# The last of sixteen token blocks finished in two halves, with new orders for the last two blocks

## The chip, the cores and the metric

The kernel runs on one core of a Trainium2 chip, in one launch. The metric is the device time of an execution in microseconds (us); smaller is better. Engines are named as the profile names them: PE is TensorE (matrix products and transposes), PEld its weight loads, DVE is VectorE, ACT is ScalarE, POOL is GpSimd, and SP issues the plain DMAs.

## The reference

The input x is 128 sequences of 64 tokens with 256 features. Four residual steps follow one another:

```python
x = x + attention(x, cond)        # 16 heads, keys = queries = values from one projection, modulated by cond
x = x + adapter(x, cond)          # returns up + its input, so this step gives 2 x + up
x = x + fuse(x, ids, cond, ...)   # layer norms with per-token tables, W1 (silu), W2, layer norm
x = x + decoded(x, cond)          # per sequence: x @ (U V) + bias, U (256 x 30) decoded from cond
```

The change touches the end of the third step and the fourth step:

```python
h = jax.nn.silu(s @ W1 + b1) @ W2 + b2
return _ln(h, g, b)               # added to x, which then goes through the fourth step
...
out = jnp.einsum('bsd,bde->bse', x, weight) + bias[:, None, :]
```

All arithmetic of these parts is in fp32.

## The kernel before, in words

**Blocks and tiles.** The 8192 tokens are cut into 16 blocks of 512 tokens (8 sequences), numbered 0 to 15, each of 4 tiles of 128 tokens. Each block goes through `attention` (lines 842 to 993, with `tile_attention` for each tile) and then `rest` (1177 to 1464). Several things are kept transposed, features by tokens: x1T after attention (line 986), x2T after the adapter (1222).

**What `rest` does.** The adapter is two groups of small products (`down`, 1191, and `up`, 1209). Each tile of x2T is transposed back to tokens by features (1259, 1262), normalized (statistics 455 and 456 on DVE; one over the root and the offset on POOL, 460, 462, 1239 and 1240; the normalization itself on ACT, 1245), scaled by a gathered table (1270, 1276), normalized again, and transposed (1294, 1297). Per-token tables are put in through one-hot products (1303, 1312). W1 is 16 products of 512 columns for a block (1330) and one of a table (1339), then silu (1345, 1348), which leaves s2, features by tokens.

From here on the change is at work. W2 gives one product for each tile of 128 tokens (`second`, 1373): DVE adds b2 (1378) and takes the statistics (455, 456); POOL makes ry = (variance + epsilon) to the power -1/2 and nry = - mean times ry for all four tiles at once (460, 462, 1239, 1240); ACT normalizes each tile (1245); POOL scales it and adds x2 (1384, 1387). For the fourth step the normalized tiles are transposed (`turn`, 1399) for each half c of the features. In all blocks but the last an ACT copy with a bias makes x3T of it. In the last block, `quick` is set: the transposes read the normalized tile yn before POOL's scaling, and a DVE scalar_tensor_tensor scales, adds x2T and writes x3T (1405), so that POOL's scaling is beside this path and not on it. `first` (1426) multiplies x3T by the decoded U of each sequence, DVE adds ub and writes zT (1437), `last` (1452) multiplies by V, DVE adds x3 (1460), and SP stores 128 tokens at a time (1464).

**The order of the work.** A planner (class `Plan`, lines 59 to 202) collects all operations of the whole kernel with a guessed duration, their inputs and outputs and the buffers they need, and then lays them out with a list schedule: at each step it takes, on each engine, those operations that could start first (within 0.02 us of the earliest), and of these the one with the smallest number; the emitted program follows this order on every engine. The number comes from a table for each kind of block (`TURNS`, 208 to 308: "prologue", "first", "second", "middle", "last but one", "last"), one number for each operation in the order in which the code lists them, plus 400 for each block:

```python
            picks = []
            for eng, c in best.items():
                first = min(c)[0]
                picks.append(min(((p, n, t) for t, p, n in c if t <= first + 0.02)))
            t, n = min((t, n) for _, n, t in picks)
```

The block before its own `rest` is over shares the engines with the attention of the next block, so the tables of blocks 14 ("last but one") and 15 ("last") decide how the last two blocks lie beside each other. Nothing follows block 15. PE results go to four banks of accumulator memory (kind "bank") and one group of four banks for attention scores. An operation with a new buffer can only be placed when a buffer of that kind is free.

Of the kernel before, what the change touches and what calls it, by code (L numbers as in the profile page):

```python
# [12 lines left out]
AF = mybir.ActivationFunctionType  # L13
ALU = mybir.AluOpType
# [4 lines left out]
C = 2  # L19
T = 512  # L20
# [38 lines left out]
class Plan:  # L59
# [177 lines left out]
    -16938 -30526 -18028 36301 -15547 26405 -802 6729 -39099 -41863 42240 -45014 -14562 -27174 17926 -11891 -33252  # L237
    -15193 -45201 -45201 -45201 -12582 9703 17987 22744 15597 -18168 17424 -28042 -41758 -7357 -451 25437 -8991
    -12614 459 -11776 29958 -7569 23567 -6641 13097 26814 -28106 7375 -575 12318 20069 -38198 23459 -38462 36836
    27311 31943 -4776 26854 -14776 2811 12753 3636 -20535 28655 16056 22892 -31515 6510 -3096 -41775 12301  # L240
    """,
    "second": """
    13400 17649 -18056 -2478 -39796 -25603 -43400 19336 -42575 -24634 15841 18877 1893 18958 3437 12808 907 8003
# [11 lines left out]
    1457 -45077 -25320 -34934 -8032 -37786 -19094 -8437 5339 5339 5339 -12394 -20304 14994 3721 -11664 -7635 -27664  # L255
    27176 20895 26121 9336 -35791 -14043 -7673 8369 -42327 -31969 -25693 17291 2553 -36411 -3402 -15873 13422 7027
    -32778 19435 22712 -20010 12141 -39669 -37660 1149 -27222 -44023 37623 -37115 -18717 26495 3505 18710 -32292 -430
    15236 18791 21609 -17410 29738
    """,
    "middle": """  # L260
    -945 -5006 28741 3275 -555 -2679 4333 19756 13246 29462 3507 42603 5115 -1489 14772 22434 -2133 33481 31798 41815
# [9 lines left out]
    25821 12505 -1402 -5360 3342 27949 30405 6793 33874 -4408 26737 -9042 5014 33335 43087 44838 12803 42849 4251  # L271
    28780 21150 7584 9227 29132 5260 5260 5260 28987 31520 -2237 3828 8090 938 30118 3864 -4871 -7133 4057 30319
    11418 -2268 -597 -6095 7699 -2331 11788 11039 36273 619 1024 4669 34043 16725 5303 33221 -6438 31026 14080 11161
    37456 23037 11095 -11007 27922 -5110 11858 21714 35520 -1388 28909 27611 779 30000 -4851 23042
    """,
    "last but one": """
    -945 -5006 28741 3292 -555 -2679 4333 19756 13246 29426 3507 42507 949 -1489 14772 22434 -2092 33522 31798 41815
    951 30003 36734 39833 31441 44287 36835 36712 48388 -2211 33995 35152 6414 18014 27987 -10794 26523 6071 13167
    215 -9627 40936 -4357 6419 10572 4571 -7266 41550 17576 2454 32076 31767 -2728 16615 41208 837 4340 8765 36154
    -10880 4665 -558 -2062 4662 -3798 1273 31044 36706 35521 -1668 -419 19391 3818 26245 31507 24910 28317 -6286  # L280
    26998 -11618 25996 12900 26677 40415 20947 4197 4591 -10897 34316 29621 46596 6494 -4361 -5325 30488 28382 33266
    18048 33066 30258 -4468 44044 39446 3045 11442 54 3568 3791 -5774 -2389 836 17585 32107 3610 3509 11677 27998
    5918 -289 -3076 10611 22471 8317 24462 31609 27367 -11407 5640 5006 25531 6317 12721 12013 -6353 39363 7446 4072
    -1182 -2303 33420 5842 -3197 -3385 30659 31515 868 756 5023 33464 5290 34805 27086 29256 -2628 -4019 6625 33507
    3780 1799 30520 32280 29029 46575 20997 32367 9369 29333 -3611 1761 5073 23038 -2673 4124 -3837 18828 -210 5311
    32964 13572 -5042 815 27152 -6571 45385 6618 32189 18218 25530 13431 4354 28866 27343 42996 27711 28905 48852
    20499 25821 12505 19373 -5371 3342 27949 30404 6752 33874 -4408 26737 -9042 5014 33335 43087 44864 12794 42849
    4268 28770 21167 7601 9132 29149 5277 5277 5277 29004 31538 -2220 3845 8107 955 30135 3881 -4854 -7113 4074 30336
    11443 -2251 -580 -6078 4549 -2314 4266 11515 36765 1109 1500 5145 34519 17201 5779 33709 -5975 31030 14097 11178
    37473 23054 11112 -11491 27939 12681 11926 21735 35542 -1369 28928 27461 806 30077 -4774 23069  # L290
    """,
    "last": """
    -918 -4932 28785 3332 -569 37576 95 19583 13303 29612 3564 42657 5172 -1432 14778 22470 -2127 33487 31798 41753
    970 30025 36750 39866 31463 44309 36857 36734 48399 29838 33987 35461 6445 18036 28009 -10772 26548 6113 13077
    237 -9611 40952 -4341 6378 10566 11434 -7289 41527 17553 -2664 32185 32004 -2665 16815 41408 1037 4540 8965 36354
    -10831 4624 -604 -2085 4601 -3493 1256 17026 36681 35506 -1449 -434 19376 3801 25885 18811 24911 28352 -6303
    26981 -11699 25941 12883 26660 40398 20930 37525 4574 -10945 34299 29411 46591 6473 3726 -5383 30451 28410 33294
    18120 33105 30216 -4508 44002 39404 2964 11361 -166 3348 3579 -5994 -2333 610 18563 31899 3363 3325 4560 27779
    5744 -463 -3063 10622 -5376 8328 24473 31758 33518 -11396 5316 4677 43337 5936 12777 11684 -6037 39679 7352 3989
    -1170 -2067 33534 5696 -3081 -3304 30916 3513 1082 969 -1348 33586 5412 34403 27208 29378 -11701 -4005 6612 27354  # L300
    3767 1811 -9041 32275 33374 46570 20992 32362 9366 29381 -3588 1701 5121 4398 17015 4312 -3658 31671 -173 5447
    33077 13685 12794 -1508 27373 -6586 45375 6606 32445 18219 25520 13404 4325 28839 16940 42969 36247 29019 48820
    20465 25794 12337 -1583 -5541 3161 27768 30224 6612 33693 -4589 26551 -9304 4752 33073 42825 44576 12454 42500
    3902 28515 20894 7574 8848 28753 4872 4872 4993 28720 31263 -2335 3579 7833 -1601 29984 3730 -5005 -7186 4016
    30266 11356 -2321 -666 -6056 7806 -2377 11778 11029 36263 589 994 4678 34088 16701 5288 33069 -6488 30973 13881
    11108 37403 22984 11042 -11060 27869 3313 11805 21661 19322 -1441 28856 27558 772 29993 -4858 10564
    """,
}

# [2 lines left out]
def resid_chain(ctx: ExitStack, tc: tile.TileContext, a: dict, out: bass.AP, nblk: int = NBLK):  # L312
# [13 lines left out]
    def over_tokens(ap):  # L326
        return ap.unsqueeze(len(ap.shape)).to_broadcast([*ap.shape, S])
# [105 lines left out]
    def pe(us, f, reads, writes, claims=(), full=1.0, mode=0):  # L433

        op("PE", us + 0.16, f, reads, writes, busy=us, claims=claims, full=full, mode=mode)

    def dve(n, f, reads, writes, more=0.0, pair=False):

        us = 0.085 + n / 960 + more
        op("DVE", us + 0.08, f, reads, writes, busy=us, pair=pair)  # L440

    def act(n, f, reads, writes, more=0.0, table=0):
        us = 0.085 + n / 1200 + more
        op("ACT", us + 0.08, f, reads, writes, busy=us, table=table)

    def pool(us, f, reads, writes):
        op("POOL", us + 0.1, f, reads, writes, busy=us)
# [5 lines left out]
    def stats(x, mv, tl):  # L453
        st = Buf("st")
        dve(256, lambda: nc.vector.bn_stats(st.t, x.t), [x], [st])  # L455
        dve(6, lambda: nc.vector.bn_aggr(mv.t[:, tl, :], st.t), [st], [(mv, tl)])  # L456
# [538 lines left out]
    def tile_attention(b0, tl, xsT, dmk, osT):  # L995
# [178 lines left out]
            [(osT, tl)],  # L1174
        )

    def rest(blk, x1T, pw, oh, wdn, wup, tab, uT):

        b0 = blk * NB
# [62 lines left out]
        def normalize(dst, src, r, nr, tl):  # L1242
            act(
                256,
                lambda: nc.scalar.activation(
                    dst.t, src.t, AF.Identity, bias=nr.t[:, tl : tl + 1], scale=r.t[:, tl : tl + 1]
                ),
                [src, r, nr],
                [dst],
                more=0.186,  # L1250
            )
# [111 lines left out]
        else:  # L1363
            plan.skip(C)
        mvy, ry, nry = Buf("mvy"), Buf("ry"), Buf("nry")
        x3 = [Buf("x3") for _ in range(NTILE)]
        yn = [Buf("h") for _ in range(NTILE)] if quick else x3
        for tl in range(NTILE):
            ps = Buf("bank")

            def second(ps=ps, tl=tl):
                for c in range(C):
                    nc.tensor.matmul(  # L1373
                        ps.t[:, :F], s2.t[:, c, bass.ts(tl, 128)], w2.t[:, c, :], start=(c == 0), stop=(c == C - 1)
                    )
# [4 lines left out]
        rstd(mvy, ry)  # L1380
        offset(mvy, ry, nry)
        for tl in range(NTILE):
            normalize(yn[tl], x3[tl], ry, nry, tl)
            pool(0.65, lambda tl=tl: nc.gpsimd.tensor_tensor(x3[tl].t, yn[tl].t, lg, ALU.mult), [yn[tl]], [x3[tl]])
            pool(
                0.65,
                lambda tl=tl: nc.gpsimd.tensor_tensor(x3[tl].t, x3[tl].t, x2[tl].t, ALU.add),
                [x3[tl], x2[tl]],
                [x3[tl]],
            )  # L1390
# [3 lines left out]
        for c in range(C):  # L1394
            ps = Buf("bank")

            def turn(ps=ps, c=c):
                for tl in range(NTILE):
                    nc.tensor.transpose(ps.t[:, bass.ts(tl, 128)], yn[tl].t[:, bass.ts(c, 128)], ident)  # L1399

            pe(0.5, turn, yn, [ps], [x3T])
            if quick:
                dve(
                    512,
                    lambda ps=ps, c=c: nc.vector.scalar_tensor_tensor(
                        x3T.t[:, c, :], ps.t, lgT[:, c : c + 1], x2T.t[:, c, :], ALU.mult, ALU.add
                    ),
                    [ps, (x2T, c)],
                    [(x3T, c)],
                )  # L1410
                continue
            act(
                512,
                lambda ps=ps, c=c: nc.scalar.activation(x3T.t[:, c, :], ps.t, AF.Identity, bias=lbe[:, c : c + 1]),
                [ps],
                [(x3T, c)],
                more=0.093,
            )
# [171 lines left out]
```

## Time and profile before

| | us |
|---|---|
| median of 3 runs | 899.68 |
| lowest and highest | 899.44, 901.99 |
| the profiled execution, its own time | 902.43 |
| its span, from the first to the last instruction | 900.6 |
| mean granted clock of TensorE | 0.985 |

| engine | busy us | share of the span | instructions |
|---|---|---|---|
| PE | 832.6 | 92% | 9752 |
| DVE | 636.7 | 71% | 1365 |
| POOL | 608.1 | 68% | 826 |
| ACT | 447.6 | 50% | 825 |

The profile belongs to the execution of 902.43 us, so times from its start and durations are compared with its span of 900.6 us; 1.8 us lie outside. The busy times of PE are modelled, and its instructions overlap at their ends. A product in fp32 stands as two PE instructions in the trace. "idle before <- X" names the instruction whose end released a waiting one. The tile names in the trace are those of the memory: x2, x3, h and xn live in slots that show as "uu" or "p", x3T and s2 show as "uu", and b2, lg and vw as "late".

### The profile page before, as it was taken

How to read it: one execution, taken by the hardware profiler on the slowest of the kernel's cores; microseconds unless marked ns; L12 is line 12 of the kernel's file. 1: busy time of each engine (PE TensorE's matmuls, PEld its weight loads, DVE VectorE, ACT ScalarE, POOL GpSimd, SP SyncE). 2: the span in 40 equal slices, each digit the busy share in tenths (PEclk: the TensorE clock that was granted, in tenths of full speed). 3: DMA queues.
4: the chain of work that ended last, by engine and by line, in shares of the span. 5: the costliest groups of instructions: out<-in, count | busy, mean ns of one | idle time of the engine just before them, and what ended most of it. 6: DMA issues, size and time to landing. Idle time of an engine off the chain costs nothing.

```text
span 900.6 us, 23967 instructions
## 1 busy us (share of the span) xinstructions
PE 832.6 (92%) x9752; PEld 535.5 (59%) x9752; DVE 636.7 (71%) x1365; ACT 447.6 (50%) x825; POOL 608.1 (68%) x826
## 2 busy tenths in 40 slices
PE   5869999999999999999999999999999999999884
PEld 3648746656665756656565746656565757565442
DVE  3679867768685877777685868777685858776543
ACT  1454453545564555555455645555454645545241
POOL 4463673949687695949496794949496786945333
PEclk9989999999999999999999999999999999999997
DMA  8768742133423242332324232322324222202000
GB/s 264 191 151 237 253 122 77 56 86 107 126 84 116 68 122 76 94 95 76 116 83 128 66 112 81 92 94 73 115 84 128 77 85 66 82 3 71 1 24 25
DMA packets 62575, 90.24 MB, mean 100 GB/s; under 512 B 6328, under 2 KB 46200, under 8 KB 62464
## 3 DMA queue, kind: packets, MB, share of 16 engines
q1 hardware_dynamic: 57344, 71.92, 27.9%
q0 software_dynamic: 5120, 16.78, 6.0%
q8 instruction: 77, 1.26, 0.6%
q14 instruction: 34, 0.28, 0.1%
HBM read 75.44 MB, written 13.24 MB: 98 GB/s over the span
## 4 chain that ended last, share of the span: by engine, by line
PE 76%; DVE 10%; ACT 7%; issue 3%; POOL 2%; DMA 2%; SPq 0%; DVEq 0%; ACTq 0%; POOLq 0%
PE bank L1330 21%; PE sc L1057 8%; PE bank L1001 7%; PE bank L968 6%; PE bank L1373 6%; PE bank L1132 6%; DVE mt L1066 4%; PE bank L1044 2%; PE sc L1107 2%; PE bank L1162 2%; ACT uu L1297 2%; PE bank L1209 2%; PE bank L1399 2%; PE bank L1303 2%; PE bank L1191 2%
## 5 line engine op out<-in xcount | busy, mean ns | idle before, releaser
L1066 DVE TENSOR_REDUCE mt<-sc 128x8 f32<-128x1024 f32 x128 | 151.8, 1205 | 27.8 <-PE sc L1057 25.3
L1121 ACT ACTIVATE e<-sc 128x1024 f32<-128x1024 f32 x128 | 125.8, 1022 | 78.8 <-PE sc L1107 78.8
L1151 POOL TENSOR_TENSOR att<-ao,rz 128x256 f32<-128x256 f32 x45 | 28.0, 623 | 83.3 <-DVE rz L1148 77.3
L1312 DVE TENSOR_TENSOR uu<-uu,bank 128x512 f32<-128x512 f32 x96 | 63.6, 678 | 14.3 <-PE bank L1303 13.9
L1001 PE MATMUL bank<-wk,xsT 128*128 128x256 f32 x256 | 72.7, 420 | 1.1 <-POOL xsT L911 1.1
L1330 PE MATMUL bank<-uu,w_s 128*128 128x512 f32 x128 | 66.7, 604 | 0.8 <-DVE uu L1312 0.8
L1330 PE MATMUL bank<-x2T,w_x 128*128 128x512 f32 x128 | 64.7, 608 | 0.0
L1330 PE MATMUL bank<-uu,w_t 128*128 128x512 f32 x128 | 63.4, 604 | 0.5 <-DVE uu L1312 0.5
L1373 PE MATMUL bank<-w,uu 128*128 128x256 f32 x256 | 61.8, 385 | 1.9 <-DVE uu L1348 1.9
L1001 PEld LDWEIGHTS bank<-wk,xsT 128*128 128x128 f32 x256 | 49.8, 206 | 20.1 <-issue 11.0
L968 PE MATMUL bank<-osT,wo 128*128 128x512 f32 x128 | 59.2, 604 | 0.5 <-DVE osT L1167 0.5
L1330 PE MATMUL bank<-uu,w_h 128*128 128x512 f32 x128 | 58.7, 595 | 0.5 <-DVE uu L1312 0.4
L1076 ACT COPY mt<-mt 128x16 f32<-128x16 f32 x64 | 13.1, 204 | 90.1 <-DVE mt L1066 89.6
L460 POOL TENSOR_SCALAR ry<-mvy 128x4 f32<-128x4 f32 (+1 forms) x19 | 4.4, 232 | 76.7 <-DVE mvy L456 76.6
L455 DVE BATCH_NORM_STATS2 st<-uu 128x6 f32<-128x256 f32 x119 | 48.4, 417 | 7.8 <-ACT uu L1262 4.7
L1015 POOL TENSOR_TENSOR kxe<-kxe,kbr 128x256 f32<-128x256 f32 x64 | 46.7, 730 | 8.0 <-DVE kxe L1009 5.5
L1373 PEld LDWEIGHTS bank<-w,uu 128*128 128x128 f32 x256 | 45.9, 190 | 9.4 <-DVE uu L1348 3.1
L1009 DVE TENSOR_TENSOR kxe<-bank,dmk 128x256 f32<-128x256 f32 x64 | 26.8, 419 | 31.4 <-PE bank L1001 28.1
L942 POOL TENSOR_TENSOR wdn<-gdb,late 128x512 f32<-128x512 f32 x32 | 40.7, 1275 | 11.2 <-PE bank L1191 6.1
L926 POOL DMA_INDIRECT pw<-in_pw,idx x39 | 40.0, 1025 | 8.1 <-issue 7.5
L956 POOL TENSOR_TENSOR wup<-wup,ubb 128x512 f32<-128x512 f32 x32 | 40.6, 1267 | 3.5 <-DMA ubb<-ugub 1.4
L1089 ACT ACTIVATE mX<-bank,early 128x128 bf16<-128x128 f32 x64 | 23.5, 367 | 38.9 <-PE bank L1082 38.8
(205 smaller groups left out, 2127.7 us busy)
## 6 DMA issues: line engine op xcount, KB each, us to landing
xT<-in_xT SPq DMA_DIRECT2D x32, 256.0 KB
gdb<-dgdb SPq DMA_DIRECT2D x16, 512.0 KB
ubb<-ugub SPq DMA_DIRECT2D x32, 256.0 KB
wup<-ugub SPq DMA_DIRECT2D x32, 256.0 KB
dmk<-demod_k SPq DMA_DIRECT2D x30, 256.0 KB
out_x<-uu SPq DMA_DIRECT2D x35, 128.0 KB
ud<-uu SPq DMA_DIRECT2D x8, 512.0 KB
uT<-ud SPq DMA_DIRECT2D x16, 256.0 KB
```

Source lines behind the costliest of these rows:

```text
L455: dve(256, lambda: nc.vector.bn_stats(st.t, x.t), [x], [st])
L942: lambda w=w, dp=dp: nc.gpsimd.tensor_tensor(w(), gdb.t[:, :, 0:64], dp, ALU.mult),
L968: nc.tensor.matmul(ps.t, owT[:, c, bass.ts(oc, 128)], osT.t[:, c, :], start=(c == 0), stop=(c == C - 1))
L1001: nc.tensor.matmul(ps.t[:, :F], xsT.t[:, c, bass.ts(tl, 128)], kwT[:, c, :], start=(c == 0), stop=(c == C - 1))
L1015: lambda: nc.gpsimd.tensor_tensor(kxe.t[:, :, 0:D], kxe.t[:, :, 0:D], heads(kinds["kbr"][0]), ALU.add),
L1057: nc.tensor.matmul(sc.t[:, q, bass.ts(g, 128)], of_g(kT.t)[r, g, :], of_g(kR.t)[r, g, :], start=(g == 0), stop=(g == 3))
L1066: lambda two=two: nc.vector.tensor_reduce(mt.t[:, two, 0:4], sc.t[:, two, :].rearrange("p q (g n) -> p q g n", g=4), AX.X, ALU.max),
L1121: lambda k=k: nc.scalar.activation(es[k].t, sc.t[:, 2 * k : 2 * k + 2, :], AF.Exp, scale=0.25),
L1132: nc.tensor.matmul(ps_o.t[32 * q : 32 * q + 32, bass.ts(g, 128)], v.t.rearrange("p (g q d) -> p g q d", g=4, q=4)[:, g, q, :], es[q // 2]. ...
L1312: lambda ps=ps, src=src, dst=dst, c=c: nc.vector.tensor_tensor(dst.t[:, c, :], src.t[:, c, :], ps.t, ALU.mult),
L1330: lambda ps=ps, w=w, src=src, fc=fc, c=c, n=n: nc.tensor.matmul(ps.t, w.t[:, c, bass.ts(fc, 128)], src.t[:, c, :], start=(n == 0 and c == ...
L1373: nc.tensor.matmul(ps.t[:, :F], s2.t[:, c, bass.ts(tl, 128)], w2.t[:, c, :], start=(c == 0), stop=(c == C - 1))
```

## The change

The last block calls a new function `finish` in place of the end of `rest`; the branches for `quick` behind that point go. `finish` runs everything from W2 on for tiles 0 and 1 and for tiles 2 and 3 apart: statistics on POOL over two columns, transposes of two tiles into a bank, a scalar_tensor_tensor of 256 columns, `first` for 4 of the 8 sequences, the add of ub on 64 of 128 partitions, one `last`, two adds and two stores. The code lists half 0 first; which one leads is left to the planner's numbers. The block's number of operations goes from 272 to 282. All numbers of "last but one" and "last" are new; in "first", "second" and "middle" the last number is only repeated to the new length.

The diff, with the tables cut to their ends:

```diff
     "last but one": """
-    -945 -5006 28741 3292 -555 -2679 4333 19756 13246 29426 3507 42507 949 -1489 14772 22434 -2092 33522 31798 41815
...
+    86709 43797 -22164 13420 -9686 -46973 -73669 -12029 -22673 -13454 62889 -19244 -16937 84228 153232 17546 -40841
...
     "last": """
-    -918 -4932 28785 3332 -569 37576 95 19583 13303 29612 3564 42657 5172 -1432 14778 22470 -2127 33487 31798 41753
...
+    -22953 -44621 -13765 -32044 -7483 28539 53922 4502 33460 -56009 -154600 111971 -4844 -50159 -69635 20107 -31146
...
+    -42251 2687 23081 174991 -51534 44112 -6285 200520 -22379 -62805 -61040 16727 122448 -82281 -33606 38675 16185
+    -51633 41485 138455 118123 -127018 19771 176553 19136 70453 221546 11677 -13398 -71835 87180 -24141 92052 71038
+    188535 -3854 100758 46400 36510 -30591 203649 152311 -57102 53052 -185143 -65966 98017 -113148 -36822 4296 -30436
+    -154799 14253 -40028 -179610 79392 -35982 26259 287 24248 -43575 21896 -106418 32662 972 203384 102121 54002
+    17711 50776 -119128 36915 132001 67228
     """,
...
+    def finish(blk, s2, x2, x2T, uT, mvy, ry, nry):
+
+        x3, yn = ([Buf(k) for _ in range(NTILE)] for k in ("x3", "h"))
+        x3T, zT = Buf("s2"), Buf("zT")
+        for half in range(2):
+            tiles = 2 * half, 2 * half + 1
+            of = slice(2 * half, 2 * half + 2)
+            for tl in tiles:
+                ps = Buf("bank")
+
+                def second(ps=ps, tl=tl):
...
+                pe(0.88, second, [s2, w2], [ps], [x3[tl]])
+                dve(256, lambda ps=ps, tl=tl: nc.vector.tensor_tensor(x3[tl].t, ps.t[:, :F], b2, ALU.add), [ps], [x3[tl]])
+                stats(x3[tl], mvy, tl)
+            mine = [(mvy, tl) for tl in tiles]
+            r, nr = ry, nry
+            pool(
+                0.25,
+                lambda of=of: nc.gpsimd.tensor_scalar(r.t[:, of], mvy.t[:, of, 1], EPS_LN, None, ALU.add),
...
+            pool(
+                0.8,
+                lambda of=of: nc.gpsimd.tensor_tensor(r.t[:, of], r.t[:, of], mhalf[:, of], ALU.pow),
...
+                lambda of=of: nc.gpsimd.tensor_scalar(nr.t[:, of], mvy.t[:, of, 0], -1.0, None, ALU.mult),
...
+                lambda of=of: nc.gpsimd.tensor_tensor(nr.t[:, of], nr.t[:, of], r.t[:, of], ALU.mult),
...
+            for tl in tiles:
+                act(
+                    256,
+                    lambda tl=tl: nc.scalar.activation(
+                        yn[tl].t, x3[tl].t, AF.Identity, bias=nr.t[:, tl : tl + 1], scale=r.t[:, tl : tl + 1]
+                    ),
...
+                pool(0.65, lambda tl=tl: nc.gpsimd.tensor_tensor(x3[tl].t, yn[tl].t, lg, ALU.mult), [yn[tl]], [x3[tl]])
+                pool(
+                    0.65,
+                    lambda tl=tl: nc.gpsimd.tensor_tensor(x3[tl].t, x3[tl].t, x2[tl].t, ALU.add),
...
+            cols = bass.ts(half, T // 2)
+            for c in range(C):
+                ps = Buf("bank")
+
+                def turn(ps=ps, c=c, tiles=tiles):
+                    for n, tl in enumerate(tiles):
+                        nc.tensor.transpose(ps.t[:, bass.ts(n, 128)], yn[tl].t[:, bass.ts(c, 128)], ident)
+
+                pe(0.26, turn, [yn[tl] for tl in tiles], [ps], [x3T])
+                dve(
+                    256,
+                    lambda ps=ps, c=c, cols=cols: nc.vector.scalar_tensor_tensor(
+                        x3T.t[:, c, cols], ps.t[:, : T // 2], lgT[:, c : c + 1], x2T.t[:, c, cols], ALU.mult, ALU.add
+                    ),
...
+            ps = Buf("bank")
+
+            def first(ps=ps, half=half):
+                for q in range(2):
+                    for c in range(C):
+                        for j in (2 * half, 2 * half + 1):
+                            b = 2 * j + q
+                            nc.tensor.matmul(
+                                ps.t[32 * j : 32 * j + 32, bass.ts(q, S)],
...
+            pe(0.3, first, [uT, (x3T, (0, half)), (x3T, (1, half))], [ps], [zT], full=0.43, mode=2)
+            rows = slice(64 * half, 64 * half + 64)
+            dve(
+                128,
+                lambda ps=ps, rows=rows: nc.vector.tensor_tensor(
+                    zT.t[rows, :].rearrange("p (b t) -> p b t", t=S),
+                    ps.t[rows, :128].rearrange("p (b t) -> p b t", t=S),
+                    over_tokens(ub3.t[rows, blk, :]),
...
+            pso = [Buf("bank") for _ in range(2)]
+
+            def last(pso=pso, half=half):
+                for i in range(2):
+                    rr = slice(64 * half + 32 * i, 64 * half + 32 * i + 32)
+                    nc.tensor.matmul(pso[i].t[:, :F], zT.t[rr, :], vw[rr, :], start=True, stop=True)
+
+            pe(0.5, last, [(zT, half)], pso, full=0.43, mode=1)
+            for i, tl in enumerate(tiles):
+                n = blk * NTILE + tl
+                dve(
+                    256,
+                    lambda tl=tl, ps=pso[i]: nc.vector.tensor_tensor(x3[tl].t, ps.t[:, :F], x3[tl].t, ALU.add),
...
+                load(128, 1024, lambda tl=tl, n=n: nc.sync.dma_start(out=out[bass.ts(n, 128), :], in_=x3[tl].t), [x3[tl]], [])
...
         mvy, ry, nry = Buf("mvy"), Buf("ry"), Buf("nry")
+        if quick:
+            finish(blk, s2, x2, x2T, uT, mvy, ry, nry)
+            return
         x3 = [Buf("x3") for _ in range(NTILE)]
-        yn = [Buf("h") for _ in range(NTILE)] if quick else x3
```

## The prediction

> **What bounds the kernel now.** I read the stages first: busy time of each engine over stretches of the span. (Columns: stretch and length; busy us of PE, PEld, DVE, ACT, POOL with their instructions; granted TensorE clock; DMA share; GB/s.)
>
> ```profile
> 700.00:800.00 100.00, 97.04 (x1209) 62.48 (x1208) 74.18 (x162) 53.99 (x98) 74.46 (x100) 1.00 0.24 70
> 800.00:881.40 81.40, 71.50 (x735) 40.17 (x734) 47.70 (x110) 36.37 (x68) 37.59 (x63) 1.00 0.09 27
> ...
> 881.43:885.20 3.77, 3.72 (x16) 2.96 (x16) 2.56 (x9) 0.00 (x0) 0.00 (x0) 1.00 0.00 0
> ...
> 890.30:900.60 10.30, 3.92 (x46) 2.28 (x45) 3.29 (x7) 0.01 (x1) 4.17 (x7) 0.50 0.17 54
> ```
>
> Until 800 TensorE is the bound: idle 2.96 us in 100. From 800 to 881.4, where only blocks 14 and 15 are left, it is idle 9.90 us; at the earlier rate it would be 2.41, so 7.5 us is the most that a better order of these two blocks could win there. From 881.4 on nothing is full, and TensorE runs at half clock in the end: that stretch is one chain. The chain of waits in order of time shows it (start, length, what):
>
> ```profile
> 881.43 3.73 PE bank L1373 x16
> ...
> 886.38 0.23 POOL ry L460
> ...
> 886.92 1.01 POOL ry L462
> 887.93 0.07 issue
> 888.00 0.21 POOL nry L1240
> 888.21 0.02 issue
> 888.24 0.61 ACT uu L1245
> ...
> 891.73 0.76 DVE uu L1405
> 892.50 0.04 issue
> 892.54 0.91 PE bank L1426 x24
> 893.45 0.02 issue
> 893.48 0.30 DVE zT L1437
> 893.78 0.04 issue
> 893.82 1.30 PE bank L1452 x8
> ```
>
> All four tiles of W2, then one statistics step on POOL, then four normalizations, and so on: each step waits for all four tiles of the step before. The last add ends at 896.65 and the last store is issued at 897.06; the span ends 3.54 us after that.
>
> **The change, part 1: the end in halves.** I write times from the start of W2 (881.43 = 0). Before, these are: statistics chain on POOL from 4.95, first normalization 6.81, last one done 8.88, last add done 15.22, last issue 15.63, end 19.17.
>
> Which half goes first is read from the new table: its last 58 numbers belong to the 58 operations of the halves in the order of the code. For the four W2 products they are 16185, 118123, -65966, 4296, and the smaller goes first among what is ready: tiles 2, 3, 0, 1. So half 1 leads.
>
> *First half.* W2's products end every 0.87 us, as now; DVE's adds start at 1.17, 2.04, 2.90, 3.76 (rows of line 1378 in the timeline). The second tile's aggregate starts now at 3.24 and ends at 3.41, so POOL begins at 3.50 in place of 4.95. POOL: epsilon 0.23, negation 0.31 after it, power 0.20 after that at 4.01. The power over 128x2 is in no row; over 128x1 it is 0.585, over 128x4 1.04 (line 462), so I interpolate to 0.74, to 4.75; product at 4.83, normalization at 5.07, two of them to 6.15 (0.60 and 0.49 more). That is 1.74 earlier than 6.81.
>
> *Second half.* Its statistics end as now, 4.95, so its POOL chain runs from 5.05 (behind the first half's product, to 5.03): power 5.56 to 6.30. Then POOL has a choice: the first half's scaling (line 1384's kind, 0.73) has been ready since about 5.74, while the chain's product must wait 0.08 for the power. The planner starts what is ready first, so I let one scaling slip in: product at 7.03, normalization at 7.28, both done at 8.36. Before, four were done at 8.88. From the last normalization to the first scalar_tensor_tensor it is 0.57 now (890.31 to 890.88, transposes at half clock); kept: 8.93. This DVE step over 256 in place of 512: 0.42 (the 256-wide adds) in place of 0.80; the other half of the features waits for two more transposes at 0.23, so 9.40, done 9.85. Twelve of 16 first products after it: 0.91 x 12 / 24 = 0.46, with its start 10.35; the ub add 0.30, at 10.38 to 10.68; the last products: 0.82 from start to add at full clock in block 14 (860.72 to 861.54), 1.30 for twice as many here; I take 1.1 between them: 11.80. Two adds, 0.37 apart: done 12.6.
>
> *What is late next.* POOL: eight scale and residual operations at 0.69 spacing (0.72 or 0.73 each) for both halves, and the second chain between them. From 6.30: one scaling, the product 0.21, seven more: 0.73 + 0.21 + 7 x 0.69 = 5.77, to 12.1; the last add then runs 12.15 to 12.57. Both paths end at 12.6, so POOL has no slack left, where today it ends at 13.1 against an add at 13.7.
>
> *Added work and what hides it.* Four statistics operations on POOL and a shorter second power: 0.23 + 0.23 + 0.21 + 2 x 0.74 - 1.04 = 1.11, already in the sums above. DVE: 4 x 0.42 against 1.60, and one more ub add (0.29): 0.37, of which the first half's share lies beside the second half's POOL chain. TensorE has the same products and transposes in twice the groups, and four banks serve them as now. POOL covers nothing more: one operation of 0.7 us too many there is 0.7 at the end. SP: the stores of the first half leave during the second half; only two are queued at the end, so the last issue follows its add by 0.04 (as the first store now, 895.58 to 895.62) instead of 0.41.
>
> Sum: last issue 12.64, plus 3.54 = 16.2 against 19.17: **-3.0 us**. Its ends: -3.1 if the chain's product isn't held up, for then POOL alone still lasts to 6.38 + 0.21 + 8 x 0.69 = 12.1 and the last add to 12.5; -1.0 if all four POOL operations of the first half go ahead of the second half's product (4 x 0.69 in place of one, 0.73: 2.0 later).
>
> The clock: TensorE is idle from 885.20 to 888.89, 3.69 us, and the granted clock is 0.5 from about 887.8 to the end, through 3.92 busy us in the 10.3 that follow 890.3. With halves the gap is only some 2.0 us (3.72 to about 5.7). I keep half clock, because the end has not been seen to leave it.
>
> The Trainium skill, "TensorE: Matmul & The Clock Gate", Part 1, says that the clock falls after an idle window of about 3.4 us, in windows that run free of the kernel. This trace's fall during a 3.69 us gap agrees. By that rule the shorter gap could keep full speed for both halves' transposes and products, an estimate of 1 us less on TensorE; but POOL's 12.1 would then set the end, and the sum would be -3.1 in place of -3.0. No run so far shows a 2.0 us gap followed by light work.
>
> **Part 2: the new order of blocks 14 and 15.** No row prices an order. From one side, the 7.5 us of excess idle time are the limit. It lies where block 15's own chain has nothing beside it: TensorE waits 1.31 for x1T (line 1191, 852.27), 0.83 for att, 0.52 for osT, 0.48 for act, and later 0.64, 0.78 and others for normalized tiles. Block 14's W1 (16 products, 32 instructions at 0.43, 13.8 us) runs from 820 to 838.5, before block 15's attention is done (850.7); moved behind it, it would fill these gaps. In the new tables the mean number of TensorE's operations is about 24000 for block 14 and 11000 for block 15 (before: 15500 and 15100), a lean towards block 15 first, which is this direction. From the other side, the same 13.8 us can be put in front: half of it (6.9) ahead of block 15's attention makes all that follows 6.9 later. The bounds are -7.5 and +6.9; the lean speaks for the gain, the numbers are scattered by tens of thousands on both sides and speak for little of it: I take **-1.5**, one fifth of what is there.
>
> **Total:** span 900.6 - 4.5 = 896.1; the profiled execution 902.43 - 4.5 = 897.9. That execution lies 2.75 above the median of the runs, so the forecast for the median is 899.68 - 4.5 = **895.2**.
>
> **Rivals.**
>
> - *Order worth nothing:* halves alone, -3.0: 896.7. For it: the idle gaps are links of a serial chain (x1T, att, osT), which an order doesn't shorten.
> - *Order worth much:* -4.5 of the 7.5, with -3.0: 892.2. For it: 13.8 us of movable W1. Against: it needs banks, four in all, while attention wants them too.
> - *The halves fall together again:* POOL takes the first half's four operations before the second half's product, -1.0, order nothing: 898.7. For it: POOL is full from 5.7 on. Against: the power starts before any of them is ready.
> - *Slower:* W1's 6.9 us of block 14 ahead of block 15's last attention tiles; x1T of block 15 comes at 859 instead of 852.2. 899.68 + 6.9 - 3.0 = 903.6. It decides from a delay of 5.7 us (3.0 of gain and 2.7 of the bound below). Against: the lean of the tables.
>
> **How the numbers follow.** Forecast (893.7 to 896.2) 0.45; order worth nothing (896.2 to 897.7) 0.22; order worth much 0.10; halves together 0.10; slower 0.13. A measurement tells 0.3% from no change, 2.7 us: faster is below 897.0. Faster: 0.45 + 0.10 + 0.13 of the second case = 0.68; same 0.09 + 0.10 = 0.19; slower 0.13. The range leaves out the slower case and the lowest third of the much-gain case: 891.5 to 899.5.
>
> **What would show it.** In the changed profile: W2 in two groups with POOL's statistics starting about 3.5 us after the first product; normalizations in two pairs about 2 us apart; from the start of block 15's W2 to the end of the span 16.2 us (19.2 before); POOL nearly without a gap before the last adds; the two last stores 0.4 apart. For the order: W2 of block 15 starts at about 879.9, and TensorE's idle time from 800 to there is about 8.4. Wrong is the forecast if that start lies beyond 881.4, or if the end takes more than 17.5 us.

## The result, and the profile after

In the first comparison the changed kernel took 897.99 us (median of 12 runs, 892.84 to 901.35) against 900.18 for the kernel before (12 runs, 898.42 to 902.76): ratio 0.9972, 95% interval 0.995 to 0.9993. In two later comparisons, on two chips, the same pair gave 1.0011 (0.9997 to 1.0024) and 1.0007 (0.9993 to 1.0021). So the changed kernel was 0.3% faster in one comparison, and the two others show no difference that can be told from none. The profiled execution of the changed kernel took 894.69 us, span 892.9; that of before 902.43, span 900.6. How much of these 7.7 us belongs to the change is the first question.

The stages of the changed kernel (columns as in the prediction; the first two rows are cut at the same times as before, the other two at the same points of the work):

```profile
700.00:800.00 100.00, 97.11 (x1190) 61.95 (x1187) 72.68 (x160) 53.55 (x98) 72.84 (x99) 1.00 0.22 65
800.00:875.26 75.26, 65.58 (x633) 36.30 (x632) 40.78 (x97) 31.49 (x61) 34.02 (x57) 1.00 0.10 29
875.31:878.66 3.35, 3.29 (x14) 2.58 (x14) 2.58 (x9) 0.00 (x0) 0.24 (x1) 1.00 0.00 0
882.05:892.90 10.85, 5.57 (x44) 3.26 (x44) 3.33 (x9) 1.09 (x2) 4.76 (x7) 0.50 0.15 51
```

TensorE is idle for 9.68 us between 800 and s2 (75.26 - 65.58); before it was 9.90 between 800 and W2. But this execution is ahead, so 800 is a later point of its work. From the point that lies as far behind block 13's first adapter product as 800 did before (793.2 to 875.26, 82.06 us with 72.19 busy), it is idle for 9.87 us. No gap has been filled. POOL's statistics now begin within W2's stretch (x1), not after it. The changed kernel's chain of waits shows the two halves:

```profile
875.31 2.44 PE bank L1197 x10
...
878.92 0.68 POOL ry L1214
...
879.67 0.21 POOL nry L1226
...
881.95 1.25 PE bank L1271 x16
883.20 1.05 PE bank L1253 x4
884.25 1.15 PE bank L1297 x4
885.40 1.02 PE bank L1271 x16
...
886.79 1.27 PE bank L1297 x4
```

The first statistics step comes after 12 of W2's 16 instructions (two ran before s2, ten behind it), where it came after all 16. Lines 1271, 1253 and 1297 are `first`, `turn` and `last` of `finish`: `last` of the first half (884.25) stands ahead of `first` of the second (885.40), and `last` takes 1.2 us twice, where before one group of eight took 1.30.

**Where the two executions differ.** The emitted programs are the same, but for line numbers, until about 19 us after block 12's adapter starts (on DVE, ACT and POOL the first difference lies at 725 us before and 717 changed). I therefore read from each trace the start of the first adapter product (`down`) of blocks 12, 13, 14 and 15, the end of the last silu product (s2 complete) and the end of the span. Up to block 12 the changed kernel was already 7.88 us ahead (698.15 against 706.03): in 12 blocks of the same instructions. From there to the end the two took the same, within 0.15 us:

| kernel (us) | 12 to 13 | 13 to 14 | 14 to 15 | 15 to s2 | 12 to s2 | s2 to end | 12 to end |
|---|---|---|---|---|---|---|---|
| before | 49.37 | 50.07 | 45.15 | 30.76 | 175.35 | 19.27 | 194.62 |
| changed | 50.47 | 50.12 | 44.58 | 31.93 | 177.10 | 17.66 | 194.77 |

The end gained 1.61 and the way to it lost 1.75. This table, made for every run below, tells more than the times, which vary by 4 to 11 us among the 12 or 13 runs of one kernel in one comparison.

### The profile page after: what moved, and what is told of

It is laid out like the page before. It is cut to its first block, busy times and chain, and to the rows that moved or that the text cites. A ratio compares the mean times of both kernels' runs of the same rounds, so it can differ in the third digit from the quotient of the medians.

```text
span 892.9 us, 23977 instructions
## 1 busy us (share of the span) xinstructions
PE 828.7 (93%) x9752; PEld 533.5 (60%) x9752; DVE 637.5 (71%) x1368; ACT 447.2 (50%) x825; POOL 609.6 (68%) x830
## 4 chain that ended last, share of the span: by engine, by line
PE 59%; POOL 14%; DVE 12%; ACT 8%; issue 5%; DMA 2%; SPq 0%; DVEq 0%; ACTq 0%; POOLq 0%
PE bank L1463 18%; PE sc L1065 6%; PE bank L1009 5%; PE bank L1140 4%; PE bank L1508 4%; PE bank L976 4%; DVE mt L1074 3%; PE sc L1115 2%; PE bank L1052 2%; PE bank L1436 2%; PE bank L1170 2%; ACT uu L1430 1%; ACT e L1129 1%; ACT uu L1378 1%; PE bank L1427 1%
## 5 line engine op out<-in xcount | busy, mean ns | idle before, releaser
L1445 DVE TENSOR_TENSOR uu<-uu,bank 128x512 f32<-128x512 f32 x96 | 63.6, 678 | 18.0 <-PE bank L1436 17.5
L1009 PE MATMUL bank<-wk,xsT 128*128 128x256 f32 x256 | 69.6, 406 | 1.2 <-POOL xsT L919 1.2
L1009 PEld LDWEIGHTS bank<-wk,xsT 128*128 128x128 f32 x256 | 47.9, 198 | 19.2 <-issue 11.1
L1508 PE MATMUL bank<-w,uu 128*128 128x256 f32 x240 | 57.6, 384 | 0.8 <-DVE uu L1481 0.8
L1508 PEld LDWEIGHTS bank<-w,uu 128*128 128x128 f32 x240 | 43.1, 190 | 6.9 <-DVE uu L1481 1.0
```

The lines of the kernel that those rows point to most:

```text
L1009: nc.tensor.matmul(ps.t[:, :F], xsT.t[:, c, bass.ts(tl, 128)], kwT[:, c, :], start=(c == 0), stop=(c == C - 1))
L1445: lambda ps=ps, src=src, dst=dst, c=c: nc.vector.tensor_tensor(dst.t[:, c, :], src.t[:, c, :], ps.t, ALU.mult),
L1508: nc.tensor.matmul(ps.t[:, :F], s2.t[:, c, bass.ts(tl, 128)], w2.t[:, c, :], start=(c == 0), stop=(c == C - 1))
```

## The experiments

In each row the stretches come from one profiled execution, and the ratio from all runs of that kernel against those of the kernel before on the same chip. The first four rows ran on one chip, the next four on a second, the last four on a third.

| run (us) | 12 to 13 | 13 to 14 | 14 to 15 | 15 to s2 | s2 to end | 12 to end | ratio to before (95%) |
|---|---|---|---|---|---|---|---|
| e1 changed again | 50.46 | 50.01 | 44.56 | 31.92 | 17.66 | 194.62 | 1.0011 (0.9997 to 1.0024) |
| e2 halves, old order | 49.21 | 49.21 | 45.14 | 30.75 | 18.47 | 192.79 | 0.9994 (0.9979 to 1.0009) |
| e3 whole, new order | 50.46 | 50.01 | 44.56 | 31.94 | 18.73 | 195.70 | 1.0017 (1.0002 to 1.0032) |
| e4 before again | 49.20 | 49.22 | 45.14 | 30.75 | 19.27 | 193.58 | 0.9995 (0.9978 to 1.0011) |
| e5 `last` behind `first` | 49.36 | 50.08 | 45.13 | 30.75 | 18.20 | 193.53 | 1.0001 (0.9984 to 1.0017) |
| e6 and POOL's chain first | 49.39 | 50.10 | 45.14 | 31.92 | 18.26 | 194.81 | 1.0001 (0.9985 to 1.0017) |
| e7 block 14's new numbers | 50.48 | 49.13 | 51.17 | 45.19 | 18.86 | 214.84 | 1.0232 (1.0211 to 1.0254) |
| e8 block 15's new numbers | 49.42 | 49.91 | 52.63 | 31.91 | 18.74 | 202.61 | 1.0086 (1.0066 to 1.0107) |
| e9 old order, new end | 49.43 | 49.39 | 45.15 | 30.75 | 17.65 | 192.38 | 0.9976 (0.9959 to 0.9994) |
| e10 whole, W2 turned | 49.39 | 50.09 | 45.14 | 30.75 | 18.85 | 194.22 | 0.9995 (0.9979 to 1.0011) |
| e11 ends together | 49.37 | 50.08 | 45.14 | 33.73 | 17.76 | 196.08 | 0.9982 (0.9968 to 0.9995) |
| e12 changed, third time | 50.46 | 50.09 | 44.56 | 31.93 | 17.66 | 194.70 | 1.0007 (0.9993 to 1.0021) |

### Halves and order apart (e1 to e4)

e1 and e4 are the two kernels unaltered. e2 has the new function and the old numbers, e3 the old function and the new numbers:

```diff
 e2, on the changed kernel
-    "last but one", "last": the new numbers
+    "last but one", "last": the old numbers, each operation of a half with the number it had as a whole
 e3, on the kernel before
-    "last but one", "last": the old numbers
+    "last but one", "last": the new numbers, shared operations with those of the first half
```

> The changed kernel once more, unaltered. I measure from the first adapter product of block 12 (the last landmark before the two programs part) to the second silu product of block 15 (s2 complete) and from there to the end of the span. In the two profiles at hand: before 175.3 and 19.2, sum 194.6; changed 177.1 and 17.6, sum 194.7. Theory A, the halves gain 1.6 and the new order costs 1.7 upstream: again about 177 and 17.6. Rival B, the order is worth nothing or a little, and the 1.7 belongs to that one execution, as the 0.7 us steps do that differ between the two profiles in blocks where the programs are the same: 175.5 or less, and 17.6. Time against the kernel before: 0.997 by the runs so far; both theories allow it.

> Halves alone: the new function with the old numbers for blocks 14 and 15 (each operation of a half takes the number of the operation it came from). A: 175.3 upstream and 17.6 at the end, sum 193.0, 1.7 faster than the changed kernel. B: sum as the changed kernel's, within 0.7. My prediction's own part 1 would have 16.2 at the end.

> The new numbers alone: the end of the last block whole as before, with the new numbers (operations that are shared by the halves take those of the first half). A: 177.1 upstream and 19.2 at the end, sum 196.3, 1.7 slower than before. B: 175.3 or less upstream and 19.2, within 0.7 of before. The prediction's part 2: 173.8 upstream.

> The kernel before, unaltered, as its own control: ratio 1.000, and from block 12 on 175.3 and 19.2 again under A; under B the upstream stretch may differ by about 1 us between executions of this same program.

Theory A holds: with the new numbers the way to s2 takes 177.0 on this chip in both functions, with the old 174.3 in both. The new order costs 2.65 us here (1.75 in the first pair). B is right in one term: 13 to 14 was 50.07 in one execution of the kernel before and 49.22 in another, and across all runs with the old order it is near 49.2 or near 50.1, so this term proves nothing. The other three are within 0.25 us of each other in all executions of one order, but for the last term of e6 and e11, which are taken up below: 12 to 13 loses 1.1 to 1.25, 15 to s2 loses 1.17, and 14 to 15 wins 0.57. The end: halves alone 0.80 (e2), the new numbers alone 0.54 (e3), both 1.61.

What TensorE waits for from block 15's adapter to s2 shows most of the loss of the last stretch: 4.1 us in e4 and 5.0 in e1 (rows of W2 itself left out). First e4 (old order), then e1 (new order):

```profile
...
PE bank L1191 <- DVE x1T L986: 1.3, 1, 1.3
PE bank L1330 <- DVE uu L1312: 1.1, 2, 0.8
PE bank L1294 <- ACT x2T L1358: 0.6, 1, 0.6
PE bank L1209 <- ACT act L1200: 0.5, 1, 0.5
PE bank L1259 <- DVE x2T L1222: 0.4, 1, 0.4
PE bank L1303 <- ACT uu L1297: 0.2, 1, 0.2
```

```profile
PE bank L1463 <- DVE uu L1445: 1.5, 2, 1.2
PE bank L1324 <- DVE x1T L994: 1.3, 1, 1.3
PE bank L1436 <- ACT uu L1430: 0.9, 1, 0.9
PE bank L1534 <- POOL uu L1522: 0.8, 1, 0.8
...
PE bank L1342 <- ACT act L1333: 0.5, 1, 0.5
```

The wait for x1T, which I hoped an order would fill, is 1.3 in both. New is 0.8 for `turn` of block 14 (line 1534), which waits for POOL, and 0.7 more for line 1436. The chain of the changed kernel says what is queued behind that `turn`:

```profile
844.98 1.37 POOL uu L1519 x2
846.35 2.06 POOL uu L1522 x3
...
848.46 0.67 PE bank L1534 x4
...
849.15 0.46 ACT uu L1539
...
850.31 0.38 ACT uu L1395
```

POOL's scaling and residual adds of block 14 (1519, 1522) hold back its transposes on TensorE, these hold ACT's copies of block 14 (1539), and behind those stand ACT's copies of block 15's x2 (1395), the head of the chain to s2. From block 15's first adapter product to the first of these copies it is 6.99 us (843.32 to 850.31), before 6.22 (850.62 to 856.84): 0.77 of the 1.17. Where the other 0.40 goes was not followed. Nor was the loss from 12 to 13: TensorE's waits there add to 1.0 us in e4 and 1.6 in e1, which is 0.6 of the 1.25.

### One block's numbers at a time (e7, e8)

```diff
 e7, on the kernel before:  "last but one": old numbers -> new numbers
 e8, on the kernel before:  "last": old numbers -> new numbers
```

> Before, with the new numbers for block 14 alone. Upstream is 174.3 with the old numbers and 177.0 with the new, in executions on the same chip: 49.2, 49.2, 45.1, 30.8 from the first adapter product of block 12 to those of 13, 14 and 15 and to s2, against 50.5, 50.0, 44.6, 31.9. Theory A, that block 14's numbers carry the first two terms: 50.5, 50.0, and the rest as before, sum 1.5 to 2.1 above before. Rival B, that block 15's numbers do: 49.2, 49.2.

> Before, with the new numbers for block 15 alone (operations that are shared by the halves take those of the first half). Theory A: the first two terms as before, 49.2 and 49.2, the last 31.9 in place of 30.8, the end 18.7 in place of 19.3, sum 0.6 above before. Rival B: the first two terms rise here.

The first term goes with block 14's numbers (50.48 against 49.42), as A has it. In e8 the last term (31.91) and the end (18.74) also came as A has them; but 3.41 us of that term ran at half clock, so its agreement shows little. Neither theory had the rest: 14 to 15 took 51.17 and 52.63 us in place of 45.14, with 10.2 and 6.8 us of it at half clock, and 15 to s2 took 45.19 in e7. Numbers of the two blocks are compared with each other whenever both have something ready, so one table of a pair does not have half of the pair's effect but makes another order altogether: 21.3 and 9.1 us more from block 12 on than the mean of e4 and e5 (193.56). The longest wait in e7 from block 14's adapter on:

```profile
PE bank L1401 <- POOL uu L1389: 9.5, 1, 9.5
```

Transposes of block 14 stood in TensorE's queue for 9.5 us, until POOL had scaled block 14's tiles and added the residual, with all of block 15 behind them. It is the same mechanism as the 0.8 us above, twelve times as large, and the granted clock fell to half for 17 us after it.

### The order at the end (e5, e6)

In e2 the end took 18.47, not the 16.2 of the prediction. TensorE's queue had the first half's `last` ahead of the second half's second transposes. e5 moves it, and the code there lists both halves' `first` before either `last`; e6 also puts POOL's statistics product of the second half ahead of the scaling:

```diff
 e5, on e2 (a marker that first writes and last reads; the planner then orders them)
-            pe(0.3, first, [uT, ...], [ps], [zT], full=0.43, mode=2)
+            pe(0.3, first, [uT, ...], [ps, tok], [zT], full=0.43, mode=2)
-            pe(0.5, last, [(zT, half)], pso, full=0.43, mode=1)
+            pe(0.5, last, [(zT, half), tok], pso, full=0.43, mode=1)
 e6, on e5 (the product writes tok2, every scaling reads it)
-                [(nr, half)],
+                [(nr, half), tok2],
-                pool(0.65, ... lg, ALU.mult), [yn[tl]], [x3[tl]])
+                pool(0.65, ... lg, ALU.mult), [yn[tl], tok2], [x3[tl]])
```

> Halves with the old numbers, and on TensorE the last products of the first half put behind the first products of the second half. In the run with the halves and the old numbers, TensorE took the first half's last products (1.23 us at half clock) while the second half's transposes waited behind them, and the end took 18.5. Theory A, that TensorE's queue holds the second half: the end takes 17.2, and the sum from block 12 on is 191.5. Rival B, that POOL's eight operations hold it: no more than 0.3 off 18.5.

> As the run above, and POOL takes the second half's statistics product before any scaling of the first half. Theory A: the second half's normalizations start 0.6 earlier, but POOL ends at 12.1 after s2 as before, so the end takes 16.8 at best, sum 191.1, against before 193.6 and the changed kernel 194.6: 0.987 of neither, 2.5 us (0.3%) faster than before. Rival B, that the scaling that slipped in costs nothing: as the run above.

B holds for both: 18.20 and 18.26, though in e5 the last add ended 1.46 us earlier than in e2 (13.94 against 15.40 after s2) and in e6 1.80 earlier (13.60). So neither TensorE nor the adds set the end. In e6 the clock also kept full speed through all products of the end, and that moved nothing either. The two executions from s2 on, e6 first:

```profile
877.40:889.90 12.50, 7.76 (x64) 5.41 (x64) 6.28 (x19) 2.19 (x4) 8.16 (x16) 1.00 0.01 2
889.90:895.60 5.70, 0.00 (x0) 0.00 (x0) 1.09 (x4) 0.00 (x0) 0.00 (x0) 0.51 0.27 93
```

```profile
878.50:884.30 5.80, 3.78 (x17) 3.02 (x17) 3.63 (x13) 0.72 (x2) 1.92 (x7) 1.00 0.00 1
884.35:896.70 12.35, 6.22 (x48) 3.84 (x48) 3.81 (x10) 1.42 (x3) 6.18 (x10) 0.50 0.13 44
```

All 64 matrix instructions of e6's end run at clock 1.00, in e5 48 of 65 at 0.50. The one term of e6 that is off, 31.92 from block 15 to s2 with the same order as e5, goes with a fall to half clock from 849.0 to 852.4, behind the wait for x1T; e5 has no fall there and took 30.75, which leaves 1.17 us for the fall.

### What does set the end

Among POOL's last instructions is a long drain. Its record begins while POOL's last operations still run (these are their rows, before and changed) and ends well behind them:

```profile
893.82 0.72 POOL L1387 TENSOR_TENSOR uu<-uu,p 128x256 f32<-128x256 f32 x1
```

```profile
886.08 0.73 POOL L1243 TENSOR_TENSOR p<-p,uu 128x256 f32<-128x256 f32 x1
```

The rows of POOL's drains (count, then shortest, median and longest in ns, then first and last start) and of those of SP, which come behind the stores, in the kernel before:

```profile
L1586 POOLq DRAIN  x3: 45/102/6075, 893.8 to 900.4; - x3
L1586 SPq DRAIN  x3: 7/7/7, 899.2 to 900.1; - x3
```

In the changed kernel, in its third execution (e12), and in e2:

```profile
L1711 POOLq DRAIN  x3: 45/102/7323, 884.8 to 892.6; - x3
L1711 SPq DRAIN  x3: 7/7/7, 891.1 to 892.4; - x3
```

```profile
L1711 POOLq DRAIN  x3: 45/102/7320, 889.1 to 896.9; - x3
L1711 SPq DRAIN  x3: 7/7/7, 894.6 to 896.7; - x3
```

```profile
L1707 POOLq DRAIN  x3: 45/102/6075, 878.6 to 885.4; - x3
L1707 SPq DRAIN  x3: 7/7/7, 884.9 to 885.2; - x3
```

Before: the long drain runs from 893.8 for 6.08 to 899.9, after the stores are in (899.2). Changed: to 892.1, when the stores have been in since 891.1. In all 14 traces the drain ends 5.32 after POOL's last operation (894.54; 886.81), and in all but e2 the span ends 0.79 after that; only short drains and semaphores are left by then. In e2 the drain is over at 884.65, the stores are in at 884.87, and POOL's closing semaphores begin at 884.97, as if the later of the two let them go. From s2:

| kernel (us after s2) | POOL's last operation ends | last store issued | end | end less POOL |
|---|---|---|---|---|
| before, e4 | 13.17, 13.16 | 15.68, 15.68 | 19.27, 19.27 | 6.11, 6.11 |
| changed | 11.55 | 13.70 | 17.66 | 6.11 |
| e1 | 11.55 | 13.53 | 17.66 | 6.11 |
| e12 | 11.55 | 12.96 | 17.66 | 6.11 |
| e3 | 12.62 | 15.31 | 18.73 | 6.11 |
| e5 | 12.10 | 14.40 | 18.20 | 6.10 |
| e6 | 12.15 | 14.07 | 18.26 | 6.11 |
| e9 | 11.55 | 13.70 | 17.65 | 6.11 |
| e10 | 12.74 | 15.22 | 18.85 | 6.11 |
| e11 | 11.65 | 13.50 | 17.76 | 6.11 |
| e2 | 12.09 | 15.54 | 18.47 | 6.38 |

Only in e2 are the stores later: they are in 2.1 after the last issue, and the end comes 2.93 after it. The chain of waits doesn't show this: it follows the last work back, and a drain is not counted as work. In the three executions of the changed kernel the last store is issued at 13.70, 13.53 and 12.96 (e12's end ran at full clock), and the end is 17.66 each time. A run that gives POOL's last work to DVE and leaves the stores where they are wasn't made; that POOL's drain sets the end rests on this regularity in 13 of 14 traces, e7 and e8 (6.11 both) with them, and on e2, where the stores came later than POOL's drain. Why the drain lasts 5.32 us isn't shown.

### A better pair (e9 to e11)

e9 takes the old order up to s2 and the new numbers from W2 on. The new order had completed s2's first feature half first and so let W2 begin on it; the old order completes the second half first, so e9 and e10 turn W2's loop instead:

```diff
 e9, on the changed kernel: "last but one" old; "last" old up to s2, new from W2 on; and
-                    for c in range(C):
+                    for c in reversed(range(C)):
                         nc.tensor.matmul(
-                            ..., start=(c == 0), stop=(c == C - 1)
+                            ..., start=(c == C - 1), stop=(c == 0)
 e10, on the kernel before: the same turn of the loop, in the last block alone
 e11, on e9: the orders of e5 and e6, and numbers that let POOL finish tile after tile (old numbers up to s2 only, the new ones behind)
```

> Halves with the new numbers from W2 on and the old numbers for all before it (block 14 too), and W2 begins with the feature half of s2 that the old order completes first (the second; the new order completes the first one first). Theory: what the new numbers win at the end is the order of s2's two halves, 0.4 to 0.5, and TensorE's order at the end; what they lose is upstream. Then upstream is the old 174.3 to 175.4 and the end 17.7 as in the changed kernel, sum 192.0 to 193.1, 1.6 below the kernel before on the same chip (0.998). Rival, the gain at the end needs the new order upstream: the end stays at 18.2 or more.

> The kernel before, whole, with the old numbers; only W2 of the last block begins with the second feature half. Theory: the first product doesn't wait for the last silu product any more, the end takes 18.8 in place of 19.3, nothing else changes: 0.9995, not to be told from before in time, only in the trace. Rival: the add of b2 still starts 1.22 after the second product's inputs, end 19.3.

> Halves with the old numbers, W2 from the second feature half on, POOL's statistics product of the second half before any scaling, POOL's scaling and residual adds tile by tile in order, and the last products behind all first products. Theory, with the rows of the runs before: POOL ends at 11.7 after s2, the last products at 11.8, four adds and four issues to 12.9, landing 3.8: the end takes 16.7, 2.6 less than before (0.997). Rival, the four stores queue at the end and give back what the order wins: 17.7 or more.

> The changed kernel a third time, beside the three above on one chip. Theory, upstream loss and gain at the end nearly cancel: sum 194.6 to 195.5 against 193.6 to 194.6 before, ratio between 0.997 and 1.001, upstream 177, end 17.7.

e9's theory holds: the end is 17.65 without the new order upstream, and the sum 192.38 the least of all; 894.34 us against 896.26 for before and 896.96 for the changed kernel on that chip, 0.9976 (0.9959 to 0.9994). By the trace it has what the changed kernel wins at the end and loses nothing on the way to s2. The interval alone would not carry this, for the first comparison of the changed kernel gave one like it (0.995 to 0.9993) that did not come again. e10: 18.85, 0.42 less, as expected, and POOL ends 0.42 earlier. e11's theory fell: with POOL's end at 11.65, as I had it, the stores came 0.2 earlier than the changed kernel's and the end stayed at 17.76; its rival gave the right time for a reason that is wrong too, since the stores didn't set it. Its 33.73 from block 15 to s2 goes with two falls of the clock of 3.41 us each; e9 had none there. That profiled execution (902.64 us) was e11's slowest: its median of 894.69, ratio 0.9982, is close to e9's, as an end of 17.76 behind the old order would have it. e12 came out as expected.

## Why the prediction was right or wrong

The forecast was 4.5 us less; the first comparison gave 2.2 less, the later ones 1.0 more (e1's 892.34 against 891.37) and 0.7 more, and the traces from block 12 on 0.15 more, 1.04 more (e1 against e4) and about 0 (e12 against e10's way plus before's end, 194.64). The measured times fell in the range of 891.5 to 899.5, but that is luck: the medians of the kernel before differ by up to 8.8 us between comparisons (891.37 to 900.18), and in two of four they lie in the range themselves. By its own sign the forecast was wrong, for the end took 17.6 us from 875.31, more than 17.5; W2's start came before 881.4 only because this execution was 7.88 us ahead at block 12, and from there it came 1.75 later than before. Three steps did not hold.

- **Part 2, the order, -1.5: wrong in sign.** It measured +1.75 and +2.65. The lean of the mean numbers (24000 against 11000) was also misread: 11000 comes out when the new table is read by the places that operations had in the old code. By the new code's places, block 15's mean is 23900, and 13700 up to s2. Nor do means say much about the order: with one table exchanged, e7 and e8 lose 21 and 9 us. The excess idle time that I took for a store of gains was not won by this order: it is 9.9 us before and after, and its largest piece, the wait for x1T, is 1.3 us under both. The argument for "order worth nothing" was the better one; a loss that small I had only as the 6.9 us of the slower rival.
- **Part 1, the halves, -3.0: half of it.** 17.66 in place of 16.2. The first half ran as worked out: power 0.71 for 0.74, the slipped-in scaling, normalizations 2.16 apart for 2.21 (879.90 and 882.06), POOL's operations without a gap. The mis-sized terms are the second half's: `last` 1.27 for 1.1, `first` 1.02 for 0.46 (all 16 instructions, where I had 12 left), and its start held until 885.40 by the other half's `last`; the last add ended 13.55 after s2, not 12.65.
- **"The span ends 3.54 us after the last issue": wrong.** I took the step from the last store for the one that binds, because the chain of waits ends there. It was 3.6, 4.0, 4.1 and 4.7 in executions of the two kernels. POOL, which I had as equal and second (12.1), set the end, and the whole gain of 1.61 is POOL's last operation at 11.55 in place of 13.17. So my own 12.1, with the 6.11 that follow POOL, makes 18.2 and a gain of 1.0, not 3.0: this is the step that failed, and e5 and e6, with POOL's end at 12.10 and 12.15, took 18.20 and 18.26. Of the 1.61, the halves alone are 1.07 (e5; 0.80 in e2, where the stores bound it), and W2 starting on the half of s2 that is ready is 0.42 (e10), which I had nowhere in the sum. If these add up, 0.12 is left for the new numbers from W2 on.
- **Half 1 leads: wrong, and free.** The buffers of x3 are handed out in the order of the code, so in the emitted program the first half leads whatever its numbers. Nothing in the sum depended on it.
- **The clock.** It fell 6.3 us after s2 in the profiled execution, as I kept it, but at 8.0 and 12.0 in e1 and e12, the same program. The Trainium skill, "TensorE: Matmul & The Clock Gate", Part 1, has windows that run free of the kernel, and these differences agree with it. My estimate that full speed at the end would win almost nothing (0.1 us) holds: 17.66 three times. Where the chain runs through TensorE, as in e6 before s2, 3.41 us at half clock cost 1.17.

## What to carry to other kernels

Before you shorten a program's last chain, look for what the program waits for after its last work, on every engine: here it was not the last store but POOL, whose drain ends 5.3 us after its last operation, so that operation is the one to bring forward. When runs vary by more than the change is worth, cut the traces where the programs part and compare from there. Order numbers of two blocks that run beside each other work only together (e7, e8); those of a stretch that runs alone can be exchanged by themselves (e9). Judge an order by what stands in each engine's queue ahead of the chain, not by its averages, and test a new order apart from the new code.

## What the runs showed of the hardware

- POOL's drain at the end took until 5.32 us after POOL's last operation in all 14 traces, at half clock and at full, and with the last store issued 1.4 to 3.5 us after that operation.
- Identical instructions took 7.9 us longer up to block 12 in one execution than in another. 4.1 us of it come in six steps of 0.65 to 0.75 us, one in each of blocks 6 to 11, always at the same place: a reduce of the scores on DVE (line 1066) that starts some 0.7 us later behind the engine's last work in one execution than in the other (1.48 us against 0.80 in block 6), beside a gather that POOL issues. What it waits for stays open.
- Four row groups of 32 rows ran side by side in `last`: eight instructions in 1.30 us for all four tiles, and 1.27 for the four instructions of two tiles, at half clock. To halve the group saved nothing.
